# One scan instruction over two rows, with wider GpSimd products and all state groups added on GpSimd

## The chip, the cores and the metric

The kernel runs on one core of one Trainium2 chip. The metric is device microseconds of one execution; less is better. The core has a matrix engine (TensorE, PE in the profile, with its weight loads as PEld), a vector engine (VectorE, DVE), an activation engine (ScalarE, ACT), GpSimd (POOL) and SyncE (SP), which here issues the DMAs. Each engine works through its own instructions in order, and they wait for each other by semaphores. SBUF is the working memory, PSUM the memory that TensorE writes to; a PSUM bank here is 128 partitions by 512 fp32 numbers.

## The reference

A block in three steps on `x` of 4 sequences, 1024 positions and 512 features, all fp32: half a feed-forward network, a state-space layer with a selective scan, half of the same feed-forward network again. Each has a layer norm in front and a residual around it.

```python
x = x + 0.5 * ffn(layernorm(x))
x = x + mamba(layernorm(x))
x = x + 0.5 * ffn(layernorm(x))

def ffn(x):                                   # inner width 1408
    g = (x @ gate_w.T) * gate_s
    u = (x @ up_w.T) * up_s
    return ((silu(g) * u) @ down_w.T) * down_s

def mamba(x):                                 # I = 1024 channels, N = 16 states
    h, gate = split(W_in @ x)
    h = silu(causal_conv(h, 4 taps) + conv_b)
    ts, Bm, Cm = split(Wx @ h, [128, 144])    # each rms-normed
    delta = softplus(Wdt @ ts + dt_bias)
    for t in positions:                       # per channel i and state n
        s = exp(delta[t] * A) * s + delta[t] * Bm[t] * h[t]
        y[t] = sum over n of s * Cm[t]
    y = (y + D * h) * silu(gate)
    return Wout @ y
```

## The kernel before

**Tiling.** The positions are cut into 16 chunks of T = 256 (NCS = 16, four to a sequence). A chunk of the state-space layer has NI = 8 blocks of 128 channels. For the scan a block is laid out anew: S = 4 rows side by side in the free dimension, each of 128 partitions that hold 32 channels (Q = 32) times 4 states, and NS = 4 state groups g, so that 4 x 4 states of a block come to 16 rows of 256 positions. The feed-forward passes run over 512 positions at a time (the first and last over 256), in an order written out by hand (`ORDER`), and are placed between the chunks' work.

**Order of the instructions.** The program first builds a list of operations with an engine, a cost, a due time and the buffers they read and write. `Plan.run` then places them in a model of the five engines, the earliest that can start first and, among those, the one with the earliest due time (`HOT` is always first); this fixes the order on every engine and which buffer slot each one takes. Due times of chunk k come from `at(k, unit)`, with `PACE` us to a chunk and 32 units in it. `SLOTS` says how many buffers a class has: `mm` the PSUM banks of all matrix products (4), `da` the PSUM banks of the scan (3), `px` the products (14 of two rows), `rep` the spread delta and delta*h (2). One further bank, `yps`, holds the output of the fold.

**One step of the scan** (function `scan`; for each chunk k, block i, group g and pair of rows h = 0 or 2):
- ScalarE writes exp(delta * A) of each of the two rows into `da`, 128x256 each, with `A` as a pointer operand (line 841).
- GpSimd multiplies the spread delta*h with B for the pair, 128x512, into `sb` (line 848).
- VectorE runs one `tensor_tensor_scan` for each row, 128x256 (line 857), which starts from `state`, or from 0 in the first chunk of a sequence; it then copies the two last columns into `state` (line 867, not in the last chunk of a sequence) and multiplies the pair with C, 128x512, into `sb` (line 874).
- After an odd group, GpSimd adds the pair to that of the group before, 128x512 (line 882). Two summed groups for each pair of rows remain for a block.
- TensorE folds them: 8 fp32 products with a 128x32 matrix `fold` (16 instructions, as each fp32 product is two), four column groups of 32 into `yps` (line 891). VectorE adds D*h (line 903), GpSimd multiplies with the gate (line 909).

**Around it.** `normed` makes a layer norm of one tile of 128 positions: VectorE the statistics (lines 332, 333), GpSimd three small operations for 1/sqrt and the bias (lines 337 to 339), ScalarE the scaling (line 350), TensorE four transposes (line 343), ScalarE the copy out (line 358). `ffn` makes the gate and up products (line 414), whose banks ScalarE (line 429) and VectorE (line 452) empty; the down product of the full passes is split by a Strassen scheme, whose sums of halves GpSimd makes (`combine`, line 506). `prep` makes the input projection (line 633, `hp`), the four taps of the convolution (ScalarE line 668, VectorE line 676), the small projection `sp` and its rms norm (ScalarE squares line 706, GpSimd powers lines 710 to 712, VectorE line 717). `heads` makes delta (ScalarE softplus line 772, GpSimd line 784) and writes it to memory and back, spread over the partitions, by the DMAs `row` and `rep`. `gates` makes the gating products (line 633, `gp`), which ScalarE copies out (line 812). `tail` makes the output projection (line 930). Silu and softplus need other activation tables than exp, so each goes with two table loads.

Of the kernel before, what the change touches and what calls it, by code (L numbers as in the profile page):

```python
# [37 lines left out]
for _p in range(7, 14, 2):  # L38
# [3 lines left out]
SLOTS = dict(  # L42
    mm=4, da=3, rf=12, rm=6, px=14, xf=4, xi=2, xo=1, xn=3, ss=2, sm=8, sr=4, u=2, dd=2, rep=2, bc=2, sn=2, sq=1, row=8, bcd=2, tsT=1, bcT=1, xnT=1,
)
PACE = 153
# [6 lines left out]
HOT = -1e9  # L52

# [126 lines left out]
def macaron_kernel(ctx: ExitStack, tc: tile.TileContext, a: dict, out: bass.AP):  # L180
# [7 lines left out]
    yps = banks.tile([P, 2, T], F32, name="yps")  # L188
    ident = const.tile([P, P], F32, name="ident")
    make_identity(nc, ident)  # L190
    neg_half = const.tile([P, 4], F32, name="neg_half")
    nc.gpsimd.memset(neg_half, -0.5)
    fold = const.tile([P, Q], F32, name="fold")
# [40 lines left out]
    def mm(name):  # L234
        return Buf("mm", name, [P, 512])
# [44 lines left out]
    def scale_down(down, due):  # L280
        ds2 = Buf("px", "ds2", [P, 2, T])

        def flat():
            return ds2.tile.rearrange("p a t -> p (a t)")
# [35 lines left out]
    def normed(x, at_x, name, due, flipped):  # L320
        sm = Buf("sm", f"sm{name}", [P, 16])
        xn = Buf("xn", f"xn{name}", [P, H])
        tp = mm(f"tp{name}")
        m, q = (sm, 0), (sm, 1)

        def parts():
            s = sm.tile
            return s[:, 0:6], s[:, 6:8], s[:, 8:9], s[:, 9:10], s[:, 10:11]

        def spread():  # L330
            stt, mv, *_ = parts()
            pin(nc.vector.bn_stats(stt, at_x()))
            pin(nc.vector.bn_aggr(mv, stt))

        def roots():
            _, mv, ve, rs, nb = parts()
            pin(nc.gpsimd.tensor_scalar(ve, mv[:, 1:2], EPS, None, ALU.add))
            pin(nc.gpsimd.tensor_tensor(rs, ve, neg_half[:, 0:1], ALU.pow))
            pin(nc.gpsimd.tensor_scalar(nb, mv[:, 0:1], rs, -1.0, ALU.mult, ALU.mult))

        def turned():
            for k in range(KH):
                pin(nc.tensor.transpose(tp.tile[:, k * P : (k + 1) * P], xn.tile[:, k * P : (k + 1) * P], ident))

        dst, w, more = flipped
        op("DVE", 0.65, spread, x, [m], due - 9, name=f"stats{name}")
        op("POOL", 1.0, roots, [m], [q], due - 8, name=f"roots{name}")
        op(
            "ACT", 0.71,
            lambda: pin(nc.scalar.activation(  # L350
                xn.tile, at_x(), AF.Identity, bias=sm.tile[:, 10:11], scale=sm.tile[:, 9:10],
            )),
            list(x) + [q], [xn] + w, due - 4, name=f"xn{name}",
        )
        op("PE", 0.45, turned, [xn], [tp], due - 2, name=f"flip{name}")

        def out_of():
            pin(nc.scalar.copy(dst(), tp.tile.rearrange("p (k t) -> p k t", k=KH)))  # L358
            if more:
                more()  # L360

        op("ACT", 0.48, out_of, [tp], w, HOT, name=f"unflip{name}")

# [18 lines left out]
    def ffn(n):  # L382
# [13 lines left out]
        for v, (stage, p) in enumerate(of):  # L396
            x = x_of[p] if stage == 2 and p in x_of else Buf("xf", f"x{name}_{v}", [P, 2, H])
            pairs.append(x)
            for m in range(J):
                t, r = J * v + m, J * p + m  # L400
                due = ffn_due(base[0]) - FLIPS - 3 * (W4 - t)
                if x.cls == "xf":
                    src, key = (a["x"][r * P : (r + 1) * P, :], ()) if stage == 1 else (x2[r], [("x2", r)])
                    behind("xf", move(
                        lambda x=x, m=m, src=src: dma(x.tile[:, m, :], src), 256, key, quads(x, m), due - 16, after=last_of("xf"), name=x.name,
                    ))
                normed(
                    quads(x, m), lambda x=x, m=m: x.tile[:, m, :], f"{name}_{t}", due,
                    (lambda t=t: fxT[:, :, t * P : (t + 1) * P], [("fxT", t)], None),
                )  # L410
# [11 lines left out]
        for it in range(NF):  # L422
# [9 lines left out]
                [gp], [("hd", it, t) for t in ts], HOT, name=f"ungate{name}_{it}",  # L432
# [55 lines left out]
    def split_down(name, tiles, pairs, spend):  # L488
# [21 lines left out]
        for r0, r1 in ((0, 3), (3, K1)):  # L510
# [5 lines left out]
            combine(v1, a21, a22, ALU.add, h_of(r0, r1, 1) + h_of(q0, q1, 1), s_of(s1, r0, r1), n, t0 - 4 + r0, "s1")  # L516
            combine(v2, v1, a11, ALU.subtract, h_of(r0, r1, 0) + s_of(s1, r0, r1), s_of(s2, r0, r1), n, t0 + 3 + r0, "s2")
            combine(a21, a11, a21, ALU.subtract, h_of(r0, r1, 0) + h_of(r0, r1, 1), h_of(r0, r1, 1), n, t0 + 8 + r0, "s3")
# [85 lines left out]
        for r0, r1 in ((0, 3), (3, K1)):  # L604
# [3 lines left out]
                ALU.subtract, h_of(q0, q1, 0) + s_of(s2, r0, r1), h_of(q0, q1, 0), r1 - r0, t0 + 15 + r0, "s4",  # L608
# [31 lines left out]
    def prep(k):  # L640
        d = st[k]
        base = at(k - 1, 7) if k else 70.0
        xT = d["xnT"] = Buf("xnT", f"xnT{k}", [P, KH, K - 1 + T])
        for j in range(J):
# [4 lines left out]

            def edges(j=j):  # L650
# [7 lines left out]
            o = K - 1 + j * P  # L658
            normed([x], lambda x=x: x.tile, f"m{k}_{j}", base + 2 * j, (lambda o=o: xT.tile[:, :, o : o + P], [(xT, j)], None))
            op("POOL", 0.3, edges, [(xT, 1)] if j else [], [("back",)] if j else [(xT, 0), ("back",)], HOT, name=f"edges{k}_{j}")  # L660
        u = d["u"] = Buf("u", f"u{k}", [P, NI, T])
        for i in range(NI):
# [9 lines left out]
            op("ACT", 0.45, first, [hp], [(u, i)], HOT, name=f"tap{k}_{i}")  # L672
# [16 lines left out]
        sr = [Buf("sr", f"sr{k}_{j}", [P, 8]) for j in range(J)]  # L689
# [12 lines left out]
        for j in range(J):  # L702
            def squares(j=j):
                v = sp.tile.rearrange("p (j t) -> p j t", j=J)
                for q, (o, m) in enumerate(parts):
                    pin(nc.scalar.activation(sq.tile[:, o : o + m], v[:, j, o : o + m], AF.Square, accum_out=sr[j].tile[:, q : q + 1]))

            def powers(j=j):
                ss, rr = sr[j].tile[:, 0:3], sr[j].tile[:, 4:7]
                pin(nc.gpsimd.tensor_scalar(ss[:, 0:1], ss[:, 0:1], 1.0 / R, EPS, ALU.mult, ALU.add))  # L710
                pin(nc.gpsimd.tensor_scalar(ss[:, 1:3], ss[:, 1:3], 1.0 / N, EPS, ALU.mult, ALU.add))
                pin(nc.gpsimd.tensor_tensor(rr, ss, neg_half[:, 0:3], ALU.pow))

            def weigh(j=j):
                v = sp.tile.rearrange("p (j t) -> p j t", j=J)
                for q, (o, m) in enumerate(parts):
                    pin(nc.vector.scalar_tensor_tensor(
                        sn[j].tile[:, o : o + m], v[:, j, o : o + m], sr[j].tile[:, 4 + q : 5 + q], ln_w[:, o : o + m], ALU.mult, ALU.mult,
                    ))

            op("ACT", 0.6, squares, [sp], [sq, (sr[j], 0)], HOT, name=f"sq{k}_{j}")
            op("POOL", 1.4, powers, [(sr[j], 0)], [(sr[j], 1)], HOT, name=f"rr{k}_{j}")
            op("DVE", 0.54, weigh, [sp, (sr[j], 1)], [sn[j]], HOT, name=f"sn{k}_{j}")
# [82 lines left out]
    def gates(k):  # L806
        for i in range(NI):
# [5 lines left out]
                [gp], [("g", i)], HOT, name=f"ung{k}_{i}",  # L813
# [7 lines left out]
    def scan(k):  # L821
# [4 lines left out]
        for i in range(NI):  # L826
# [4 lines left out]
            for g in range(NS):  # L831
                due = at(k, i * NS + g)
                for h in range(0, S, 2):
# [3 lines left out]
                    sb = Buf("px", f"sb{nm}", [P, 2, T])  # L837
                    for j in range(2):
# [7 lines left out]
                    behind("dbu", op(  # L846
                        "POOL", 1.23,
                        lambda sb=sb, h=h, g=g, rep=rep: pin(nc.gpsimd.tensor_tensor(  # L848
                            sb.tile, rep.tile[:, h : h + 2, 1, :], bc.tile[:, g : g + 1, :].to_broadcast([P, 2, T]), ALU.mult,
                        )),  # L850
                        reps + bcs, [(sb, 0), (sb, 1)], due - 6, after=last_of("dbu"), name=f"dbu{nm}",
                    ))
                    for j in range(2):
                        key = ("state", i, g, h + j)
                        op(
                            "DVE", 0.582 if first else 0.642,
                            lambda da=da, sb=sb, j=j, h=h, g=g, b0=b0: pin(nc.vector.tensor_tensor_scan(  # L857
                                da.tile[:, j, :], da.tile[:, j, :], sb.tile[:, j, :],
                                0.0 if first else state[:, b0 + h + j, g : g + 1], ALU.mult, ALU.add,
                            )),  # L860
                            [(da, j), (sb, j)] + ([] if first else [key]), [(da, j)], due, after=last_of("scan"), name=f"scan{nm}_{j}",
                        )
                        behind("scan", plan.ops[-1])
                    if not last:
# [9 lines left out]
                        lambda sb=sb, da=da, g=g: pin(nc.vector.tensor_tensor(  # L874
                            sb.tile, da.tile, bc.tile[:, NS + g : NS + g + 1, :].to_broadcast([P, 2, T]), ALU.mult,
                        )),
                        [(da, 0), (da, 1)] + bcs, [(sb, 0), (sb, 1)], due, name=f"prod{nm}",
                    )
                    if g % 2:
                        pa = made_of[g - 1 + h // 2]  # L880
                        op(
                            "POOL", 1.23, lambda pa=pa, sb=sb: pin(nc.gpsimd.tensor_tensor(pa.tile, pa.tile, sb.tile, ALU.add)),  # L882
                            [(pa, 0), (pa, 1), (sb, 0), (sb, 1)], [(pa, 0), (pa, 1)], due + 2, name=f"both{nm}",
                        )
                    else:
                        made_of.append(sb)
# [168 lines left out]
```

## Time and profile before

| | us |
|---|---|
| median of 3 runs | 2821.67 (2821.48 to 2822.98) |
| the profiled execution | 2822.59 |
| its span | 2820.8 |
| PE busy | 2768.3 (98%) |
| DVE busy | 2543.7 (90%) |
| POOL busy | 2395.0 (85%) |
| ACT busy | 1756.3 (62%) |
| DMA engines, mean busy share by slice | 5 to 8 tenths until slice 38 |

The mean granted TensorE clock is 0.994. Instructions of one engine overlap by some tens of nanoseconds in the records, so the distance from one start to the next is a little less than the duration; busy time counts each instant once. In the groups, a line of the kernel stands with engine, operation, output and inputs, shape and count, then busy time and mean duration in ns, then the idle time before it with what ended it. The scan runs from 153 us (first exp) to about 2723 us (last sum).

The groups that the state scan consists of:

```profile
L841 ACT ACTIVATE da<-rep,a_w 128x256 f32<-128x256 f32 x2048 | 964.7, 476 | 794.8 <-DVE sb L874 734.4
L848 POOL TENSOR_TENSOR sb<-rep,bc 128x512 f32<-128x512 f32 x1024 | 1284.1, 1280 | 81.5 <-DMA rep<-row 59.2
L857 DVE TENSOR_TENSOR_SCAN da<-da,state,sb 128x256 f32<-128x256 f32 x1536 | 1090.8, 741 | 49.6 <-ACT da L841 29.5
L882 POOL TENSOR_TENSOR sb<-sb,sb 128x512 f32<-128x512 f32 x512 | 651.5, 1278 | 84.9 <-DVE sb L874 83.1
L874 DVE TENSOR_TENSOR sb<-da,bc 128x512 f32<-128x512 f32 x1024 | 692.8, 677 | 0.5
```

### The profile page before, as it was taken

To read this page: it belongs to the slowest core of one execution; us is meant where nothing else is said; L and a number is where in the kernel's file an instruction comes from. 1 tells how busy PE (TensorE), PEld (TensorE's weight loads), DVE (VectorE), ACT (ScalarE), POOL (GpSimd) and SP (SyncE) were. 2 spreads that over 40 slices of the span, in tenths; PEclk is the share of its full clock that TensorE was granted. 3 is DMA by queue.
4 is the path that set the end of the run, shared out by engine and by line. 5 is a ranking of instruction groups with operands and counts; after the bars stand their busy time and mean duration, and the time that the engine had idled before them with its cause. 6 is when DMAs were issued, how large, how long until landed. Compare 5 with 4: busy or idle time off the path is not lost.

```text
span 2820.8 us, 38816 instructions
## 1 busy us (share of the span) xinstructions
PE 2768.3 (98%) x11278; PEld 1733.2 (61%) x11278; DVE 2543.7 (90%) x5088; ACT 1756.3 (62%) x3286; POOL 2395.0 (85%) x2279
## 2 busy tenths in 40 slices
PE   8998999999999999999999999999999999999999
PEld 6565575575655755647557565575665756657458
DVE  3289899999999999999999999999999999999861
ACT  2356667667567585676666766668567576674821
POOL 1189899899898989899899999899899998989951
PEclk9999999999999999999999999999999999999999
DMA  8576667676576666866757667666676775766635
GB/s 263 168 206 178 168 184 219 185 214 197 148 236 158 202 185 172 233 160 189 206 162 236 168 185 207 196 175 194 173 224 173 219 208 153 211 165 176 175 102 155
DMA packets 304691, 531.01 MB, mean 188 GB/s; under 512 B 34016, under 2 KB 58720, under 8 KB 304480
## 3 DMA queue, kind: packets, MB, share of 16 engines
q1 hardware_dynamic: 303040, 528.35, 66.5%
q8 instruction: 90, 1.47, 0.2%
q14 instruction: 121, 0.99, 0.1%
q10 hardware_dynamic: 1440, 0.19, 0.0%
HBM read 464.84 MB, written 63.57 MB: 187 GB/s over the span
## 4 chain that ended last, share of the span: by engine, by line
PE 43%; DVE 35%; issue 7%; ACT 7%; POOL 5%; DMA 3%; SPq 0%; ACTq 0%; DVEq 0%; POOLq 0%
DVE da L857 21%; PE upf L414 11%; PE gatef L414 11%; DVE sb L874 6%; PE hp L633 3%; PE gp L633 3%; PE op L930 2%; PE paf L539 2%; POOL sb L848 2%; ACT da L841 2%; DVE u L676 2%; PE yps L891 2%; PE pcf L539 2%; DMA rep<-row 2%; PE pbf L539 1%
## 5 line engine op out<-in xcount | busy, mean ns | idle before, releaser
L841 ACT ACTIVATE da<-rep,a_w 128x256 f32<-128x256 f32 x2048 | 964.7, 476 | 794.8 <-DVE sb L874 734.4
L848 POOL TENSOR_TENSOR sb<-rep,bc 128x512 f32<-128x512 f32 x1024 | 1284.1, 1280 | 81.5 <-DMA rep<-row 59.2
L857 DVE TENSOR_TENSOR_SCAN da<-da,state,sb 128x256 f32<-128x256 f32 x1536 | 1090.8, 741 | 49.6 <-ACT da L841 29.5
L882 POOL TENSOR_TENSOR sb<-sb,sb 128x512 f32<-128x512 f32 x512 | 651.5, 1278 | 84.9 <-DVE sb L874 83.1
L874 DVE TENSOR_TENSOR sb<-da,bc 128x512 f32<-128x512 f32 x1024 | 692.8, 677 | 0.5
L414 PE MATMUL gatef<-fxT,w_gate_w 128*128 128x512 f32 (+1 forms) x1496 | 632.7, 574 | 5.1 <-ACT dd L772 3.0
L414 PE MATMUL upf<-fxT,w_up_w 128*128 128x512 f32 (+1 forms) x1496 | 624.3, 569 | 0.5 <-DVE u L676 0.5
L414 PEld LDWEIGHTS gatef<-fxT,w_gate_w 128*128 128x128 f32 x1496 | 284.5, 192 | 294.7 <-issue 267.6
L414 PEld LDWEIGHTS upf<-fxT,w_up_w 128*128 128x128 f32 x1496 | 280.9, 190 | 290.9 <-issue 268.0
L857 DVE TENSOR_TENSOR_SCAN da<-da,sb 128x256 f32<-128x256 f32 x512 | 333.5, 681 | 22.6 <-ACT da L841 19.5
L633 PE MATMUL hp<-xnT,w_W_in 128*128 128x259 f32 x1024 | 238.6, 383 | 4.3 <-ACT fxT L358 1.5
L633 PE MATMUL gp<-xnT,w_W_in 128*128 128x256 f32 x1024 | 241.1, 380 | 0.2 <-ACT fxT L358 0.2
L633 PEld LDWEIGHTS hp<-xnT,w_W_in 128*128 128x128 f32 x1024 | 192.4, 190 | 61.3 <-issue 20.1
L633 PEld LDWEIGHTS gp<-xnT,w_W_in 128*128 128x128 f32 x1024 | 191.9, 189 | 61.0 <-issue 28.4
L930 PE MATMUL op<-w_Wout,u 128*128 128x512 f32 x512 | 229.3, 594 | 0.0
L452 DVE SCALAR_TENSOR_TENSOR hd<-upf,up_s,hd 128x512 f32<-128x512 f32 (+1 forms) x187 | 131.0, 701 | 59.4 <-PE upf L414 59.4
L676 DVE SCALAR_TENSOR_TENSOR u<-hp,conv_w,u 128x256 f32<-128x256 f32 x384 | 171.9, 468 | 6.0 <-ACT u L668 5.3
L429 ACT ACTIVATE hd<-gatef,gate_s 128x512 f32<-128x512 f32 (+1 forms) x187 | 121.8, 652 | 64.0 <-PE gatef L414 63.8
L930 PEld LDWEIGHTS op<-w_Wout,u 128*128 128x128 f32 x512 | 95.8, 190 | 105.2 <-issue 99.4
L891 PE MATMUL yps<-sb,fold 128*32 128x256 f32 x2048 | 141.1, 387 | 0.6 <-POOL sb L882 0.5
L539 PE MATMUL paf<-w_half,hd 128*128 128x256 f32 x620 | 141.0, 380 | 0.0
L539 PEld LDWEIGHTS paf<-w_half,hd 128*128 128x128 f32 x620 | 117.1, 190 | 22.0 <-issue 4.4
(104 smaller groups left out, 2911.1 us busy)
## 6 DMA issues: line engine op xcount, KB each, us to landing
rep<-row SPq DMA_DIRECT2D x512, 256.0 KB, 5.0
w_half<-sd SPq DMA_DIRECT2D x272, 256.0 KB, 3.0
w_W_in<-in_W_in_dram SPq DMA_DIRECT2D x256, 256.0 KB, 3.9
w_gate_w<-in_gate_w_dram SPq DMA_DIRECT2D x187, 256.0 KB, 4.5
w_up_w<-in_up_w_dram SPq DMA_DIRECT2D x187, 256.0 KB, 3.6
row<-dd SPq DMA_DIRECT2D x128, 256.0 KB, 3.2
w_Wout<-in_Wout_dram SPq DMA_DIRECT2D x128, 256.0 KB, 3.8
bc<-bcd SPq DMA_DIRECT2D x64, 256.0 KB, 5.2
```

What stands on the lines that cost most here:

```text
L414: pin(nc.tensor.matmul(o.tile[:, :wide], lhsT=cols(w.tile)[:, k, :], rhs=fxT[:, k, :wide], start=(k == 0), stop=(k == KH - 1),))
L452: lambda up=up, it=it: pin(nc.vector.scalar_tensor_tensor(hd[:, it, :wide], up.tile[:, :wide], up_s[:, it : it + 1], hd[:, it, :wide], ALU ...
L539: pin(nc.tensor.matmul(bank.tile[:, m * hh : (m + 1) * hh], lhsT=of(r, m), rhs=w.tile[:, h * hh : (h + 1) * hh], start=(first and m == 0 a ...
L633: pin(nc.tensor.matmul(o.tile[:, :width], lhsT=cols(w.tile)[:, kk, :], rhs=xT.tile[:, kk, lo:], start=(kk == 0), stop=(kk == KH - 1),))
L676: lambda hp=hp, i=i, q=q: pin(nc.vector.scalar_tensor_tensor(u.tile[:, i, :], hp.tile[:, q : q + T], conv_w[:, i, q : q + 1], u.tile[:, i, ...
L841: lambda da=da, j=j, h=h, g=g, rep=rep, b0=b0: pin(nc.scalar.activation(da.tile[:, j, :], rep.tile[:, h + j, 0, :], AF.Exp, scale=a_w[:, b ...
L848: lambda sb=sb, h=h, g=g, rep=rep: pin(nc.gpsimd.tensor_tensor(sb.tile, rep.tile[:, h : h + 2, 1, :], bc.tile[:, g : g + 1, :].to_broadcas ...
L857: lambda da=da, sb=sb, j=j, h=h, g=g, b0=b0: pin(nc.vector.tensor_tensor_scan(da.tile[:, j, :], da.tile[:, j, :], sb.tile[:, j, :], 0.0 if ...
L874: lambda sb=sb, da=da, g=g: pin(nc.vector.tensor_tensor(sb.tile, da.tile, bc.tile[:, NS + g : NS + g + 1, :].to_broadcast([P, 2, T]), ALU. ...
L882: "POOL", 1.23, lambda pa=pa, sb=sb: pin(nc.gpsimd.tensor_tensor(pa.tile, pa.tile, sb.tile, ALU.add)),
L891: pin(nc.tensor.matmul(yps[j * Q : (j + 1) * Q, i % 2, :], lhsT=fold, rhs=made_of[2 * g + j // 2].tile[:, j % 2, :], start=(g == 0), stop= ...
L930: pin(nc.tensor.matmul(o.tile, lhsT=u.tile[:, i, j * P : (j + 1) * P], rhs=wo[i].tile, start=(i == 0), stop=(i == NI - 1),))
```

## The change

- **Scan.** The two rows of a pair become one scan of 512 columns over `da`, with 0 as its start. So that the second row does not go on from the first, the first column of each row of `da` is set to zero by a ScalarE copy (`opened`). In chunks that go on from a state, ScalarE first puts exp * state + product into the first column of `sb`, one small activation for each row.
- **Products.** GpSimd multiplies all four rows of a group at once, 128x1024. Pair sums are 1024 wide too, and one more GpSimd addition per block (`all`) adds the two sums that are left. The fold is 4 products (8 instructions) for a block, and takes a bank of class `mm`; `yps` is gone. `da` has 4 banks, `px` 8 buffers of four rows.
- **Norms.** `normed` takes two tiles at a time: VectorE adds epsilon, GpSimd makes one power for both, ScalarE makes the bias in two small activations. In `prep`, ScalarE scales the sums of squares and adds epsilon, and GpSimd makes one power for both tiles.
- **Order.** `PACE` is 150 instead of 153. The copies out of the product banks on ScalarE are due 20 us before their product's due time (`EV`) rather than first of all; the GpSimd half sums of the split down product are due 16 us earlier (`SUMS`); the output projection's matmuls are cut into four parts rather than two.

```diff
-    mm=4, da=3, rf=12, rm=6, px=14, xf=4, xi=2, xo=1, xn=3, ss=2, sm=8, sr=4, u=2, dd=2, rep=2, bc=2, sn=2, sq=1, row=8, bcd=2, tsT=1, bcT=1, xnT=1,
-PACE = 153
+SLOTS = dict(mm=4, da=4, rf=12, rm=6, px=8, xf=4, xi=2, xo=1, xn=3, ss=2, sm=6, sr=2, u=2, dd=2, rep=2, bc=2, sn=2, sq=1, row=8, bcd=2, tsT=1, bcT=1, xnT=1)
+PACE = 150
...
+SUMS = 20
+EV = 20
...
-    yps = banks.tile([P, 2, T], F32, name="yps")
...
-    def normed(x, at_x, name, due, flipped):
+    def normed(name, pair):
+        sm = Buf("sm", f"sm{name}", [P, 2, 16])
 
         def roots():
-            _, mv, ve, rs, nb = parts()
-            pin(nc.gpsimd.tensor_scalar(ve, mv[:, 1:2], EPS, None, ALU.add))
-            pin(nc.gpsimd.tensor_tensor(rs, ve, neg_half[:, 0:1], ALU.pow))
-            pin(nc.gpsimd.tensor_scalar(nb, mv[:, 0:1], rs, -1.0, ALU.mult, ALU.mult))
+            v = sm.tile
+            pin(nc.gpsimd.tensor_tensor(v[:, :, 9], v[:, :, 8], neg_half[:, 0:2], ALU.pow))
+
+        for j, (x, at_x, due, _) in enumerate(pair):
+            def spread(j=j, at_x=at_x):
+                s = sm.tile[:, j, :]
+                pin(nc.vector.bn_stats(s[:, 0:6], at_x()))
+                pin(nc.vector.bn_aggr(s[:, 6:8], s[:, 0:6]))
+                pin(nc.vector.tensor_scalar(s[:, 8:9], s[:, 7:8], EPS, None, ALU.add))
...
+            def scaled(j=j, at_x=at_x, xn=xn):
+                s = sm.tile[:, j, :]
+                pin(nc.scalar.activation(s[:, 10:11], s[:, 6:7], AF.Identity, scale=s[:, 9:10]))
+                pin(nc.scalar.activation(s[:, 11:12], s[:, 10:11], AF.Identity, scale=-1.0))
+                pin(nc.scalar.activation(xn.tile, at_x(), AF.Identity, bias=s[:, 11:12], scale=s[:, 9:10]))
...
-                [gp], [("hd", it, t) for t in ts], HOT, name=f"ungate{name}_{it}",
+                [gp], [("hd", it, t) for t in ts], due - EV, name=f"ungate{name}_{it}",
...
-            combine(v1, a21, a22, ALU.add, h_of(r0, r1, 1) + h_of(q0, q1, 1), s_of(s1, r0, r1), n, t0 - 4 + r0, "s1")
+            combine(v1, a21, a22, ALU.add, h_of(r0, r1, 1) + h_of(q0, q1, 1), s_of(s1, r0, r1), n, t0 - SUMS + r0, "s1")
...
-                    pin(nc.scalar.activation(sq.tile[:, o : o + m], v[:, j, o : o + m], AF.Square, accum_out=sr[j].tile[:, q : q + 1]))
+                    at_q = sr.tile[:, 0, j, q : q + 1]
+                    pin(nc.scalar.activation(sq.tile[:, o : o + m], v[:, j, o : o + m], AF.Square, accum_out=at_q))
+                    pin(nc.scalar.activation(at_q, at_q, AF.Identity, bias=eps, scale=1.0 / m))
...
+                sb = Buf("px", f"sb{k}_{i}_{g}", [P, S, T])
+                behind("dbu", op(
+                    "POOL", 2.31,
+                    lambda sb=sb, g=g, rep=rep: pin(nc.gpsimd.tensor_tensor(
+                        sb.tile, rep.tile[:, :, 1, :], bc.tile[:, g : g + 1, :].to_broadcast([P, S, T]), ALU.mult,
+                    )),
+                    reps + bcs, [(sb, j) for j in range(S)], due - 7, after=last_of("dbu"), name=f"dbu{k}_{i}_{g}",
+                ))
...
+                    def opened(da=da, sb=sb, h=h, g=g, b0=b0):
+                        for j in range(0 if first else 2):
+                            pin(nc.scalar.activation(
+                                sb.tile[:, h + j, 0:1], da.tile[:, j, 0:1], AF.Identity,
+                                bias=sb.tile[:, h + j, 0:1], scale=state[:, b0 + h + j, g : g + 1],
+                            ))
+                        pin(nc.scalar.copy(da.tile[:, :, 0], zeros))
+
+                    op("ACT", 0.08 if first else 0.23, opened, keys + ([] if first else hs), [(da, 0), (da, 1)] + ([] if first else hs), due - 3, name=f"open{nm}")
+                    op(
+                        "DVE", 1.12,
+                        lambda da=da, sb=sb, h=h: pin(nc.vector.tensor_tensor_scan(
+                            da.tile.rearrange("p a t -> p (a t)"), da.tile.rearrange("p a t -> p (a t)"),
+                            sb.tile[:, h : h + 2, :].rearrange("p a t -> p (a t)"), 0.0, ALU.mult, ALU.add,
                         )),
...
+            pa, pb = made_of
+            op(
+                "POOL", 2.31, lambda pa=pa, pb=pb: pin(nc.gpsimd.tensor_tensor(pa.tile, pa.tile, pb.tile, ALU.add)),
+                [(b, j) for b in (pa, pb) for j in range(S)], [(pa, j) for j in range(S)], at(k, (i + 1) * NS) + 3, name=f"all{k}_{i}",
+            )
+            yp = mm(f"yp{k}_{i}")
+
+            def summed(yp=yp, pa=pa):
+                if True:
                     for j in range(S):
                         pin(nc.tensor.matmul(
-                            yps[j * Q : (j + 1) * Q, i % 2, :], lhsT=fold, rhs=made_of[2 * g + j // 2].tile[:, j % 2, :],
-                            start=(g == 0), stop=(g == NS // 2 - 1),
+                            yp.tile[j * Q : (j + 1) * Q, :T], lhsT=fold, rhs=pa.tile[:, j, :], start=True, stop=True,
                         ))
...
-            for lo in (0, NI // 2):
-                hi = lo + NI // 2
+            for lo in range(0, NI, 2):
+                hi = lo + 2
```

## The prediction

> **What bounds the kernel now.** I read the busy times by stretch first, then the waits of each engine, then the groups by form, and last the timeline for the distance between starts. The stretch from 150 to 2700 us holds the state scan and all but the first and last matmul passes:
>
> ```profile
> core 0: us, PE busy (x) PEld busy (x) DVE busy (x) ACT busy (x) POOL busy (x), PEclk, DMA share, GB/s
> 0.00:150.00 150.00, 140.19 (x498) 92.27 (x499) 46.91 (x108) 45.86 (x75) 18.76 (x53) 1.00 0.70 216
> 150.00:2700.00 2550.00, 2511.62 (x10277) 1551.16 (x10276) 2457.78 (x4913) 1691.70 (x3179) 2346.10 (x2196) 0.99 0.68 189
> 2700.00:2821.00 121.00, 116.49 (x507) 89.74 (x505) 39.03 (x69) 18.74 (x33) 30.13 (x31) 1.00 0.42 128
> ```
>
> In those 2550 us PE is busy 98.5%, DVE 96.4%, POOL 92.0%, ACT 66.3%. PE lacks 38 us in all, and its longest single cause in that stretch is 9.9 us of waiting for POOL's half sums. So TensorE ends the stretch, with VectorE just behind; both must shrink for a gain. The other engines' waits in the same stretch:
>
> ```profile
> ACT da L841 <- DVE sb L874: 726.7, 662, 3.5
> ...
> POOL sb L882 <- DVE sb L874: 78.7, 68, 4.6
> POOL sb L848 <- DMA rep<-row: 59.2, 25, 14.7
> ...
> DVE da L857 <- ACT da L841: 49.0, 44, 4.2
> ```
>
> The columns are total us, times, longest. ScalarE waits because it runs ahead and finds no free exp bank: that is spare time. GpSimd's waits are the ones to remember, because the change loads GpSimd.
>
> **TensorE: the fold halves.** One fold is 16 matmuls now, 8 after, since the two remaining state-group sums are added on GpSimd first.
>
> ```profile
> 1226.13 1.07 PE L891 MATMUL yps<-sb,fold 128*32 128x256 f32 x16
> 1227.13 3.27 PE L414 MATMUL gatef<-fxT,w_gate_w 128*128 128x512 f32 x7
> ```
>
> Sixteen take 1.00 us from start to the next start, though one lasts 387 ns in the groups: the four column groups run side by side, in four waves. From 1.07 and 0.387 a wave is (1.07 - 0.387) / 3 = 0.23 us, so two waves last 0.62 and hold PE for 0.55. Saved: 0.45 x 128 = 58 us; if it scaled straight, 64. I take 58. The result moves from a bank of its own to one of the four that all matmuls share, for some 0.55 + 0.46 us (fold and line 903). I cost this at nothing: the other three banks take 3 x 3.5 us of gate products, 10 us of cover; without it each fold could hold PE for that 1 us, 128 us in all. PE needs 2511.6 - 58 = 2454 us; with its 38 us of idle time kept, the stretch is 2492.
>
> **VectorE: one scan for two rows.**
>
> ```profile
> 1211.47 0.68 DVE L874 TENSOR_TENSOR sb<-da,bc 128x512 f32<-128x512 f32 x1
> 1212.07 0.75 DVE L857 TENSOR_TENSOR_SCAN da<-da,state,sb 128x256 f32<-128x256 f32 x1
> 1212.73 0.46 DVE L903 SCALAR_TENSOR_TENSOR u<-u,d_w,yps 128x256 f32<-128x256 f32 x1
> ```
>
> and from the groups by form (busy, mean of one in ns, idle before it):
>
> ```profile
> L857 DVE TENSOR_TENSOR_SCAN da<-da,sb 128x256 f32<-128x256 f32 x512 | 333.5, 681 | 22.6 <-ACT da L841 19.5 <-POOL sb L848 1.2
> ```
>
> A scan with a state operand holds the engine 0.66 us, one without about 0.06 less (681 against 741 ns), 0.60. A 512-wide scan is not in the trace. Least: the slope of the plain products (677 - 418 ns for 256 columns, 1.01 ns each) gives 0.60 + 0.26 = 0.86. Most: no gain, 1.20. A 256-wide scan lasts 681 against 418 for a product, 263 more, which is a second nanosecond per column; so I take 2.05 ns, and 0.60 + 0.53 = 1.13. Pairs: 768 x (1.32 - 1.13) + 256 x (1.20 - 1.13) = 164 us saved; 347 at the least price, 92 at the most. Added: one 1-column operation per normalized tile, 96 x about 0.1 (the 99 ns between the two statistics operations) = 10. DVE falls to 2458 - 154 = 2304, 92.5% of 2492.
>
> **GpSimd: fewer, wider, but one more add.** Its form rows are 128x256 732 ns, 128x512 1284, 128x768 1825: 2.11 to 2.16 ns per column. 1024 wide is then 2.37 us, less 0.02 of overlap (1284.1 / 1024 against 1280). Now: 1284.1 + 651.5 = 1935.6. After, per block of 128 channels, 4 products, 2 pair sums and 1 last sum: 896 x 2.35 = 2106. That is +170. Roots: 102 us of three operations for each of 96 tiles become 48 powers two columns wide; one column is 571 ns, three 861, so 716 x 48 = 34: -68. The powers of the inner norm: 39.7 become 16 x 1.3 (six columns by the same slope) = 21: -19. Sum +83, so 2346 + 83 = 2429 in the stretch, **97.5% of 2492**. Two-column and six-column powers could cost from one-column to no saving; that moves 20 us.
>
> The Trainium skill (GPSIMD Engine Reference, Key points) says elementwise work is structurally about twice as fast on VectorE, and so speaks against this part. This trace agrees (1280 ns against 677 for 128x512); by the rule the last sum would sit on VectorE for about 128 x 1.2 = 154 us, with GpSimd at 2128 and VectorE at 2458.
>
> **ScalarE: the first columns.** Per pair of rows it gains a two-element copy, and in the 12 chunks of 16 that go on from a state two one-column affine operations with two pointer operands each. No such small one is in the trace. Rows: copy 366 ns, one pointer (line 772) 474, two pointers (line 668) 556, all 256 wide; line 429 gives 676 at 512 and 471 at 256, 0.80 ns per column, 205 for 256. So the fixed parts are 0.16 and 0.35 us; consecutive ones overlap 0.11 (four of line 772 take 1.57 us, so they stand 0.365 apart). Least: 768 x (2 x 0.24 + 0.05) + 256 x 0.05 = 420 us. Most, no overlap: 768 x 0.86 + 256 x 0.16 = 701. I take the least, since ACT's dependent squares already follow each other in the timeline without waiting. With 96 x 0.2 for the normalization and 96 x 0.14 for the squares, +33. ACT: 1692 + 453 = 2145, 86% of 2492; 2426 at most.
>
> The Trainium skill (ScalarE: Activation LUTs, What ACT_TABLE_LOAD costs) gives 186 ns plus 93 per pointer operand with 93 ns of overlap, from which an estimate for these operations is 527 us instead of 420. The trace's steps of 108 and 82 ns per pointer are near it; ACT would stand at 2252.
>
> A new wait comes with this: the column operation needs GpSimd's product. Behind it in ACT's queue stand the next exps and the evictions of gate, conv and gating products (lines 429, 668, 812), for which PE's four banks wait. Cover: products are due 7 us ahead of their scan, the column operation 3 us, and the banks give 10 us.
>
> **What costs nothing.** The number of DMAs is unchanged, so the rep queue on SP stays and its 59 us of GpSimd waits too. Exp banks go from three to four, which only helps ACT, that has 727 us of such waits. Paired normalization holds the first tile for the second: hidden by passes planned far ahead, but open at the end, where the flip before the last gate products follows the last add; about +1 us. The last sum lengthens the final fold by 2.3 us, under 30 us of other PE work (2727 to 2757 in the chain of waits). Priorities and pace have no price by themselves.
>
> **Sum.** The profiled run took 2822.6 (span 2820.8 and 1.8 around it), 0.9 above the median. PE alone: 2822.6 - 58 = 2765. GpSimd cannot be busy 97.5% with the waits above; VectorE shows that an engine not at the end of everything reaches 96.4% here. Between that and PE's 98.5% I take 97%: 2429 / 0.97 = 2504, 46 us less than 2550. Forecast **2777 us**.
>
> **Rivals.**
>
> *GpSimd becomes the bound and loses time (slower, 0.22).* It is in order; each pair sum waits for VectorE's last product, each gating for line 903, which now waits for a longer chain: sum, last sum, fold. It breaks even at 2429 / 2550 = 95.3%. At 94% the stretch is 2584: 2857. For it: at present it is only 92% busy, and the waits on DVE and on rep are 138 us. Against: part of those are waits of an engine that is early.
>
> *ScalarE starves the scan (slower, 0.13).* Table switches with their work block exps for 1.28 + 1.91 + 1.28 = 4.5 us, some 100 times (42 + 32 + 15 + 12). Four banks hold 4 x (1.13 + 0.06 + 0.60) = 7 us, but refilling one costs ACT 2 x 0.46 + 0.53 = 1.45 us against VectorE's 1.79, so it recovers slowly. If the small operations cost the upper 701 us, ACT needs 2426, and at a 94% share 2581 us: 2854. It decides from 95.1% upwards. Against: the 2145 I take leaves 14%.
>
> *The order keeps the waits (no change, 0.08).* PE's freed 58 us turn into waits at folds placed by a plan: 2822. Against: PE waited 0.5 us for folds' sums before.
>
> **Numbers.** Forecast case 0.57, its own range 2745 (PE also regains half of its 38 us) to 2810. Overall 2745 to 2857, the top from GpSimd at 94%. Within 0.2% is about what this kernel's runs cannot tell from no change: 0.06; faster 0.57 + 0.02 of the last rival = 0.59; slower 0.35.
>
> **What would show it.** Right: fold x8 at about 0.55 us apart, 512-wide scans 1.1 apart, PE still at 98% or more, POOL at 96 to 97.5% with fewer waits on DVE. Wrong: PE waiting for POOL's sums at folds, DVE waiting for ACT for more than 150 us, 1024-wide POOL operations above 2.45 us, small ACT operations above 0.3 apart.

## The result, and the profile after

The changed kernel takes 2898.29 us (median of 4 runs, 2895.55 to 2899.18) against 2822.32 in runs beside it: 1.0267 of the time before, 95% interval 1.025 to 1.0285. The profiled execution took 2899.18, its span is 2897.1. The forecast was 2777.

The busy times by stretch (us of each engine, number of instructions in brackets):

```profile
core 0: us, PE busy (x) PEld busy (x) DVE busy (x) ACT busy (x) POOL busy (x), PEclk, DMA share, GB/s
0.00:150.00 150.00, 139.27 (x495) 91.48 (x496) 48.72 (x119) 51.84 (x97) 9.13 (x20) 1.00 0.67 214
150.00:2780.00 2630.00, 2497.24 (x9283) 1527.62 (x9282) 2333.16 (x3993) 2264.53 (x6005) 2458.60 (x1281) 0.98 0.64 184
```

The scan's stretch has grown from about 2550 to 2630 us and no engine fills it: PE 95.0%, POOL 93.5%, DVE 88.7%, ACT 86.1%. VectorE and TensorE have less to do than before and stand idle more. The groups (busy us, mean ns, idle before them and its causes):

```profile
L872 DVE TENSOR_TENSOR_SCAN da<-da,sb 128x512 f32<-128x512 f32 x1024 | 1219.0, 1221 | 244.0 <-ACT da L867 230.7
L841 POOL TENSOR_TENSOR sb<-rep,bc 128x1024 f32<-128x1024 f32 x512 | 1209.0, 2372 | 43.6 <-DMA rep<-row 37.7
L854 ACT ACTIVATE da<-rep,a_w 128x256 f32<-128x256 f32 x2048 | 940.2, 472 | 231.5 <-DVE sb L889 207.3
...
L863 ACT ACTIVATE sb<-da,sb,state 128x1 f32<-128x1 f32 x1536 | 449.9, 343 | 42.2 <-POOL sb L841 30.0
...
L905 POOL TENSOR_TENSOR sb<-sb,sb 128x1024 f32<-128x1024 f32 x128 | 303.3, 2369 | 1.3
...
L867 ACT COPY da<-zeros 128x2 f32<-128x2 f32 x1024 | 165.3, 161 | 27.8
```

Before, scans waited 49.6 + 22.6 us in all; now 244 us, 231 of them for the column copy on ScalarE (line 867). ScalarE's own waits for a free exp bank fell from 734 to 207 us: it no longer runs ahead. In the chain of waits ScalarE now holds 33% (7% before). The scan of a pair itself takes 1.13 us from its start to that of the next operation:

```profile
1209.37 1.23 DVE L872 TENSOR_TENSOR_SCAN da<-da,sb 128x512 f32<-128x512 f32 x1
1210.50 0.47 DVE L679 SCALAR_TENSOR_TENSOR u<-hp,conv_w,u 128x256 f32<-128x256 f32 x1
```

The trace holds its own comparison. The first chunk of a sequence has no state to carry, so ScalarE does the copies there but none of the 1536 activations of line 863. The next two stretches are chunk 4, which is such a chunk, and chunk 5, which carries. Each runs from VectorE's last product with C of the chunk before to its own:

```profile
810.00:964.00 154.00, 151.46 (x544) 88.89 (x543) 147.35 (x271) 111.46 (x275) 150.48 (x80) 0.99 0.67 193
964.00:1135.00 171.00, 158.23 (x565) 92.55 (x564) 147.59 (x269) 153.47 (x416) 154.59 (x81) 0.98 0.63 180
```

Without a carry PE is busy 98.4% and GpSimd 97.7%, which is about what the prediction had asked of them; with a carry they are down to 92.5% and 90.4%. From the last product with C of one chunk to that of the next, chunks 4, 8 and 12 went from 157.2 us on average to 154.0, the eleven that carry (without the last chunk) from 162.5 to 168.4.

Of the 76 us: PE's busy time fell by 19 us only, though the fold saved 59 (141.1 to 82.1 in its row, here before and after), and PE's idle time grew by 95 (2897.1 - 2749.6 against 2820.8 - 2768.3).

```profile
L891 PE MATMUL yps<-sb,fold 128*32 128x256 f32 x2048 | 141.1, 387 | 0.6 <-POOL sb L882 0.5
```

```profile
L913 PE MATMUL yp<-sb,fold 128*32 128x256 f32 x1024 | 82.1, 392 | 21.4 <-POOL sb L905 13.2 <-ACT hd L429 2.1 <-ACT xnT L354 1.9
```

Part of the busy time that did not fall is a lower granted clock, 0.985 against 0.994: as an estimate from clock and span, 43 us missing from full speed against 17. In the place shown here it follows an idle gap:

```profile
1084.48 0.64 PE L913 MATMUL yp<-sb,fold 128*32 128x256 f32 x8
1090.53 5.66 PE L414 MATMUL upf<-fxT,w_up_w 128*128 128x512 f32 x9 [5.41 <-DVE hd L452]
```

```profile
1085.00:1090.00 5.00, 0.12 (x4) 0.00 (x0) 2.62 (x3) 4.87 (x17) 2.52 (x2) 1.00 0.65 193
1090.00:1094.00 4.00, 3.47 (x5) 1.64 (x6) 3.33 (x7) 3.95 (x8) 4.00 (x3) 0.57 0.00 0
1094.00:1100.00 6.00, 6.00 (x16) 2.65 (x15) 4.49 (x9) 5.74 (x18) 5.75 (x3) 1.00 0.44 107
```

After a gap of 5.4 us the granted clock (the number before the DMA share) is 0.57 for the next 4 us: PE pays for this stall again when it resumes. The Trainium skill (TensorE: Matmul & The Clock Gate, Part 1) says the array's clock is halved after an idle window of about 3.4 us; these rows agree. The length of the gap does not decide alone in this trace: after a gap of 2.0 us (PE resumes at 1431.11) the next 4 us had 0.57 too, and after one of 2.5 us (PE resumes at 2418.64) they had 1.00.

### The profile page after: what moved, and what is told of

It reads as the page before. It is cut to its first block, busy times and chain, and to the rows that moved or that the text cites. A ratio compares the mean times of both kernels' runs of the same rounds, so it can differ in the third digit from the quotient of the medians.

```text
span 2897.1 us, 37777 instructions
## 1 busy us (share of the span) xinstructions
PE 2749.6 (95%) x10254; PEld 1707.5 (59%) x10254; DVE 2407.8 (83%) x4160; ACT 2329.4 (80%) x6125; POOL 2492.9 (86%) x1321
## 4 chain that ended last, share of the span: by engine, by line
ACT 33%; PE 29%; DVE 20%; POOL 10%; issue 5%; DMA 3%; SPq 0%; ACTq 0%; POOLq 0%; DVEq 0%
DVE da L872 10%; ACT da L854 9%; PE upf L414 9%; ACT sb L863 6%; PE gatef L414 5%; DVE sb L889 4%; POOL sb L841 4%; ACT L1016 3%; DVE u L679 3%; POOL sb L897 2%; PE gp L633 2%; PE pcf L539 2%; PE paf L539 2%; ACT hd L440 2%; ACT hd L429 2%
## 5 line engine op out<-in xcount | busy, mean ns | idle before, releaser
L872 DVE TENSOR_TENSOR_SCAN da<-da,sb 128x512 f32<-128x512 f32 x1024 | 1219.0, 1221 | 244.0 <-ACT da L867 230.7
L841 POOL TENSOR_TENSOR sb<-rep,bc 128x1024 f32<-128x1024 f32 x512 | 1209.0, 2372 | 43.6 <-DMA rep<-row 37.7
L854 ACT ACTIVATE da<-rep,a_w 128x256 f32<-128x256 f32 x2048 | 940.2, 472 | 231.5 <-DVE sb L889 207.3
L897 POOL TENSOR_TENSOR sb<-sb,sb 128x1024 f32<-128x1024 f32 x256 | 606.7, 2370 | 74.3 <-DVE sb L889 38.1
L414 PE MATMUL gatef<-fxT,w_gate_w 128*128 128x512 f32 (+1 forms) x1496 | 641.3, 581 | 27.3 <-ACT hd L429 18.6
L414 PE MATMUL upf<-fxT,w_up_w 128*128 128x512 f32 (+1 forms) x1496 | 634.0, 575 | 20.3 <-DVE hd L452 7.4
L863 ACT ACTIVATE sb<-da,sb,state 128x1 f32<-128x1 f32 x1536 | 449.9, 343 | 42.2 <-POOL sb L841 30.0
L905 POOL TENSOR_TENSOR sb<-sb,sb 128x1024 f32<-128x1024 f32 x128 | 303.3, 2369 | 1.3
L867 ACT COPY da<-zeros 128x2 f32<-128x2 f32 x1024 | 165.3, 161 | 27.8
```

The costliest lines, as they stand in the source:

```text
L414: pin(nc.tensor.matmul(o.tile[:, :wide], lhsT=cols(w.tile)[:, k, :], rhs=fxT[:, k, :wide], start=(k == 0), stop=(k == KH - 1),))
L841: lambda sb=sb, g=g, rep=rep: pin(nc.gpsimd.tensor_tensor(sb.tile, rep.tile[:, :, 1, :], bc.tile[:, g : g + 1, :].to_broadcast([P, S, T]), ...
L854: lambda da=da, j=j, h=h, g=g, rep=rep, b0=b0: pin(nc.scalar.activation(da.tile[:, j, :], rep.tile[:, h + j, 0, :], AF.Exp, scale=a_w[:, b ...
L863: pin(nc.scalar.activation(sb.tile[:, h + j, 0:1], da.tile[:, j, 0:1], AF.Identity, bias=sb.tile[:, h + j, 0:1], scale=state[:, b0 + h + j ...
L872: lambda da=da, sb=sb, h=h: pin(nc.vector.tensor_tensor_scan(da.tile.rearrange("p a t -> p (a t)"), da.tile.rearrange("p a t -> p (a t)"), ...
L897: "POOL", 2.31, lambda pa=pa, sb=sb: pin(nc.gpsimd.tensor_tensor(pa.tile, pa.tile, sb.tile, ALU.add)),
```

## The experiments

The theory after the result: ScalarE cannot deliver the columns in time, because the plan that orders all engines was told 0.23 us for the three column operations of a pair (0.40 for an exp). In the profile the second activation starts 0.24 us after the first, the copy 0.37 us later and what follows 0.10 us later still, so that a pair takes about 0.72 us from start to start (an exp 0.40 to 0.51):

```profile
1211.55 0.59 ACT L863 ACTIVATE sb<-da,sb,state 128x1 f32<-128x1 f32 x2
1212.17 0.16 ACT L867 COPY da<-zeros 128x2 f32<-128x2 f32 x1
1212.27 0.56 ACT L671 ACTIVATE u<-hp,conv_b,conv_w 128x256 f32<-128x256 f32 x1
```

The rivals: the work itself is too much whatever the order, or GpSimd's last sum is the bound. Most experiments are single runs; where a kernel was run four or five times, the runs lie 0.1 to 0.3% apart. "True costs" below means 0.455 us for an exp and, for the column operations of a pair, 0.72 us with a carry, 0.47 with half of it and 0.10 without.

**The plan told the measured costs.** Same instructions, another order.

```diff
-                            "ACT", 0.4,
+                            "ACT", 0.455,
-                    op("ACT", 0.08 if first else 0.23, opened, ...
+                    op("ACT", 0.10 if first else 0.72, opened, ...
```

> The changed kernel with the same instructions, ordered by a plan that knows their measured distances: exp 0.455 us instead of 0.40, the column operations of a pair 0.72 instead of 0.23 (0.10 instead of 0.08 without a state). If ScalarE's work itself is the cause: 2880 to 2900 us, VectorE still waits over 180 us for the column copies. If only the order made from too low costs is the cause: 2765 to 2830 us. If GpSimd's sums are the cause: within 10 us of 2898.

2825.75 us: 73 of the 76 us are gone with no instruction changed, so the order was the main cause. VectorE's waits for the copy fell from 231 to 147 us in the scan's stretch (the columns are total us, times, longest), and PE idles 100 us of the span instead of 147.

```profile
DVE da L872 <- ACT da L867: 230.7, 158, 4.5
```

```profile
DVE da L872 <- ACT da L867: 146.5, 102, 5.0
```

> The changed kernel, with only the plan's cost of the column operations set to the measured distance (0.72 and 0.10 instead of 0.23 and 0.08); exps stay at 0.40. If that one misjudged cost makes the order bad: 2815 to 2840 us, as with both costs set (2825.8). If the exps' 0.055 us too little (2048 of them) matters as much: 2855 us or more. If any shift of the order would do: no telling, both may fall.

2834.30 us: the one number of the column operations brings 64 us of it.

> The changed kernel with the plan's exp at 0.455 us and the column operations of a pair at 1.10 us, more than the 0.72 measured. If the gain of true costs (2899 to 2826) comes from their being true: 2835 us or more, worse again. If any rearrangement, or more reserve for ScalarE, does as well: 2815 to 2830 us.

2934.63 us. A cost that is 0.38 us too high loses more than one that is 0.49 us too low, so neither just any shift of the order nor more reserve for ScalarE brings the gain. The loss is another one: VectorE's waits for the copy are down to 88 us, but PE idles 170 us of the span. Between 0.23, 0.72 and 1.10 no value was tried, so it is not shown that the measured cost is the best one.

> The kernel before, with the plan's cost of an exp 0.455 instead of 0.40 and nothing else. ScalarE has over 700 us of spare waiting there, so if misjudged costs hurt only an engine that is near full: 2815 to 2830 us. If the order gains from any truer cost: 2800 us or less.

2817.53 us beside 2822.02, the same within what single runs tell. Before the change, where ScalarE had room, an exp that was 0.055 us too cheap in the plan cost at most some 4 us.

**The parts alone.** Two scans per pair again, without the column operations; then the column copies without the carry; then the pair scan alone in the kernel before.

```diff
 # e2                       two scans of 256 columns with their start operand, no opened()
 # e3
-                        for j in range(0 if first else 2):
+                        for j in range(0):
 # e4                       the kernel before with opened() at its 0.23 us and the 512-column scan
```

> The changed kernel with the two scans per pair of before, without ScalarE's column operations; 1024-wide products, the last sum on GpSimd, four exp banks, paired norms and priorities stay. If ScalarE is the cause: 2765 to 2825 us, VectorE's waits for exps fall from 231 to under 80 us. If GpSimd is the cause: 2860 us or more, with PE waiting for the last sums.

> The changed kernel with the column copies alone: the state isn't carried into a chunk, so the 1536 one-column activations are left out. If they are the cause: every chunk takes the 154 us that the first chunks of a sequence take now, and the time falls to 2750 to 2790 us. If GpSimd is the cause: 2860 us or more.

> The kernel before with the paired scan and ScalarE's column operations alone (three exp banks, 512-wide products, the fold of 16, priorities of before). If ScalarE is the cause: 2870 to 2920 us. If GpSimd's last sum is the cause: 2780 to 2822 us, since VectorE saves some 150 us.

2817.83, 2774.83 and 2909.27 us. With two scans VectorE is the bound again, 2487.5 of 2550 us (97.5%), so that TensorE's 58 us bring only some 6. VectorE's waits for exps are down to 7 us. The paired scan with its carry costs 85 us in the old surroundings too, so neither the last sum nor the wide products are needed for the loss. Without the activations the change takes the time that was forecast (2777), even with an exp at 0.40 in the plan:

```profile
core 0: us, PE busy (x) PEld busy (x) DVE busy (x) ACT busy (x) POOL busy (x), PEclk, DMA share, GB/s
150.00:2650.00 2500.00, 2453.50 (x9267) 1517.33 (x9266) 2327.19 (x3993) 1827.38 (x4467) 2454.61 (x1281) 0.99 0.68 193
```

That is PE 98.1% and GpSimd 98.2% at once: GpSimd can be driven that full. The 1536 activations are worth 123 us in the order as changed, and 51 in the order with true costs, both against this run, whose plan makes an order of its own.

**What the remaining 51 us are.** Load, wait, or GpSimd:

```diff
 # e10: the activation writes to a place that nobody reads, without waiting for the product
-                                sb.tile[:, h + j, 0:1], da.tile[:, j, 0:1], AF.Identity,
+                                junk[:, j : j + 1], da.tile[:, j, 0:1], AF.Identity,
 # e11: no op named "all"; the fold multiplies both sums
 # e12
-PACE = 150
-SUMS = 20
+PACE = 153
+SUMS = 4
-                [gp], ..., due - EV, ...
+                [gp], ..., HOT, ...
```

> The changed kernel with both plan costs as measured; ScalarE makes all 1536 one-column activations, but writes them to a place that nobody reads and doesn't wait for GpSimd's product, so the state isn't carried. It tells ScalarE's load from its wait for the product. If the load remains the cost: 2815 to 2830 us, as with the carry (2825.8). If the wait for the product in ScalarE's queue is the cost: 2770 to 2790 us, as without the activations (2774.8).

2828.97 us: with the activations' wait for the product taken away nothing is gained, so this wait is not the cost. ScalarE's load is left as one that may be.

> The changed kernel with both plan costs as measured and without the last sum on GpSimd: the fold takes 8 products (16 instructions) again, GpSimd has 300 us less to do. If GpSimd is what keeps the version with true costs at 2826: 2800 us or less. If TensorE and ScalarE are: TensorE's 58 us come back, 2830 to 2880 us.

2812.61 us, less than with the last sum although TensorE has its 59 us of fold work back. Expected was either 2800 or less, or more than 2830; it lies between. In the scan's stretch:

```profile
150.00:2680.00 2530.00, 2494.26 (x10267) 1543.17 (x10266) 2342.34 (x3992) 2227.28 (x5985) 2168.77 (x1154) 1.00 0.68 191
```

GpSimd is down to 85.7%, ScalarE still at 88.0%, and TensorE is the bound again at 98.6%. A loaded GpSimd could be borne in e3 and a loaded ScalarE can here; that the two together are what keeps e1 from the forecast is argued from this, not shown.

> The changed kernel without the last sum on GpSimd, with the change's own plan costs (0.23 and 0.40). If ScalarE's misjudged cost is a cause by itself: 2870 us or more, some 60 above the same with true costs (2812.6). If it hurts only together with a full GpSimd: 2830 us or less.

2902.45 us, 90 more than with true costs: the misjudged costs act by themselves, with GpSimd relieved.

> The changed kernel with both plan costs as measured, and the pace, the due times of the half sums and the rank of the copies out of the product banks as before (153, 4 us ahead, first of all). If the new priorities matter: 2840 us or more. If the order is made by the costs alone: 2815 to 2835 us.

2845.95 us, 20 more than with the new priorities: with true costs these help a little, so nothing speaks for their having a part in the loss.

**Less work for ScalarE.** All three have true costs in the plan. First half of the work is taken away: the first row of a pair starts from its state in the scan, and only the second is set up. Then the whole carry of a block is made with one exp of 128x16, with the additions on VectorE (e8 and e9 are told in short, not as their code).

```diff
 # e7
-                        for j in range(0 if first else 2):
+                        for j in range(2 if first else 1, 2):
-                        pin(nc.scalar.copy(da.tile[:, :, 0], zeros))
+                        pin(nc.scalar.copy(da.tile[:, 1, 0:1], zeros[:, 0:1]))
-                            sb.tile[...], 0.0, ALU.mult, ALU.add,
+                            sb.tile[...], 0.0 if first else state[:, b0 + h, g : g + 1], ALU.mult, ALU.add,
 # e8
+                ec.tile = a_w[:, b0 : b0 + S, :] * rep.tile[:, :, 0, 0:1]     (VectorE; e9: GpSimd)
+                ec.tile = exp(ec.tile) (ScalarE; e9: into PSUM), then times state (VectorE)
+                    sb.tile[:, :, 0] += ec.tile[:, :, g]                      (VectorE, for each group)
```

> The changed kernel with both plan costs as measured, and half of ScalarE's column work: the first row of a pair starts from its state by the scan's own start operand, so that ScalarE sets up only the second row (768 activations instead of 1536, one-element copies). VectorE pays 0.06 us for 768 scans. If the remaining loss is ScalarE's work: half of the 51 us between the version with true costs and the one without a carry comes back, 2790 to 2810 us. If it isn't: 2820 us or more.

2819.24 us: 6 us better than with the whole carry, where 16 to 36 were expected. ScalarE's busy time fell by 150 us (2291.0 to 2141.1), so its load alone does not explain the 51 us.

> The changed kernel with both costs as measured, and the carry made in one go for a block: VectorE multiplies A with the first delta for all 16 rows (128x16), ScalarE makes one exp of them, VectorE multiplies with the states and adds the result to the first columns of a group's four rows; ScalarE is left with the one-element copies. If ScalarE's work is what remains: 2770 to 2795 us, as without a carry, and ScalarE below 1900 us busy. If the wait for the carry itself is what costs: 2815 us or more.

3130.01 us, far above what was expected of less work for ScalarE, and not for the reason that stood beside "2815 us or more": scans wait only 34 us. VectorE is busy 97.8% from 150 to 3000 us. The three small operations of the carry, each with both inputs in SBUF, take 337, 115 and 66 us of it. The next run moves one of them to GpSimd and gives the other two an input in PSUM:

> The batched carry again, arranged so that no VectorE operation has two inputs in SBUF: GpSimd makes the product with the first delta, ScalarE writes the exps to PSUM, and VectorE's small operations take one input from there; one exp bank fewer (3) makes the room. If VectorE's 128x4 additions took 0.9 us in the version before because GpSimd was running: they now take under 0.3 us, and the time falls from 3130 to 2770 to 2810 us. If they are slow by themselves or the order is bad: over 2850 us.

2883.68 us. The row of the addition, first with both inputs in SBUF, then with one in PSUM:

```profile
L858 DVE TENSOR_TENSOR sb<-sb,ec 128x4 f32<-128x4 f32 x384 | 337.0, 894 | 0.5
```

```profile
L860 DVE TENSOR_TENSOR sb<-sb,ecb 128x4 f32<-128x4 f32 x384 | 51.0, 159 | 49.9 <-POOL sb L854 48.3
```

894 ns became 159, and the operation of 66 us took 16.5. The time did not come down to the 2770 to 2810 expected: this version has one exp bank fewer and new waits (ScalarE 45 us for GpSimd's small product, VectorE 44 us for the wide ones), and which of them matters was not tried.

**A version that beats both.** True costs and the half carry of e7, in e16 with no last sum as in e11, in e17 with it for every other block:

```diff
 # e17
+            if i % 2:
+                op("POOL", 2.31, ... pa + pb ..., name=f"all{k}_{i}")
+                made_of = [pa]
```

> True costs, no last sum on GpSimd, and half of ScalarE's column work (the first row of a pair starts from its state in the scan). If TensorE alone bounds the version without the last sum (98.6% busy at 2812.6): 2800 to 2812 us, nothing much to gain. If ScalarE still costs: 2780 to 2800 us.

> As the run before, but the last sum goes to GpSimd for every other block: TensorE is spared 29 us, GpSimd pays 150. If the loads of GpSimd and ScalarE are what eats TensorE's 58 us: 2775 to 2800 us, the best of all that carry the state. If the last sum is bad wherever it stands: 2812 us or more.

2811.82 us, 0.9961 of the kernel before (0.9947 to 0.9975), and 2802.63 us, 0.9930 (0.9915 to 0.9945). Both gains are small, but their intervals lie below 1. In the first, with TensorE as the bound, ScalarE's relief buys nothing (2812.61 without it). The second, slightly above its expected range, trades part of TensorE's work against part of GpSimd's and is the fastest of these versions that carries the state.

## Why the prediction was wrong, by its own steps

- **The fold**: 0.62 us and 58 us forecast; 0.64 and 59 (141.1 - 82.1) measured. Right, but the time went into PE's gaps.
- **The scan**: 1.13 us from start to start forecast; the timeline has the same (1209.37 to 1210.50). VectorE's 2304 us came out as 2333 in the longer stretch. Right, though the saving at the least price was added up wrongly: 768 x 0.46 + 256 x 0.34 is 440 us, not 347. The forecast does not use that figure.
- **GpSimd**: 2.37 us forecast, 2372 and 2369 ns measured; 2429 us forecast, 2459 measured. Right. It was not thought able to be 97.5% busy; it reaches 98.2% when nothing is carried (e3).
- **ScalarE**: 0.53 us for a pair's column operations, taken at the lower bound; 0.72 measured, since the copy starts 0.37 us after the second activation instead of 0.24, and holds ScalarE for 0.10 instead of 0.05. From start to start these operations come to 768 x 0.72 + 256 x 0.10 = 579 us where 420 stood. 2145 us forecast for ScalarE, 2265 measured: too low by 120, inside the upper bound. The estimate of 527 us that the prediction worked out from the Trainium skill (ScalarE: Activation LUTs, What ACT_TABLE_LOAD costs) was nearer than 420, and low too.
- **The step that failed** is the order put at nothing ("Priorities and pace have no price by themselves"), and with it the step of the sum that rests on it, "Between that and PE's 98.5% I take 97%" for GpSimd, with ScalarE's free 14% as cover. GpSimd came to 93.5%, of 2630 us. The diff tells the plan 0.23 us for an operation that the prediction itself priced at 0.53. Against the measured 0.72, 768 of them hide some 376 us of ScalarE work from the plan, and 2048 exps at 0.40 instead of 0.455 another 113. The order then places copies, exps and evictions as if ScalarE were early. The longest wait of a scan for its copy was 4.5 us, more than the 3 us of cover. The prediction compared busy sums with the stretch and never set the plan's costs against its own. e1 and e5 show this by taking 73 and 64 us off with no instruction changed, e14 by costing 90 us with GpSimd relieved. The due times and the pace, which the sentence names, did no harm by themselves (e12).
- **What stays open**: true costs do not reach the forecast, 2825.75 us is 49 above it. Leaving out the 1536 activations brings about as much, 51, so ScalarE's free 14% was not free. Taking half of this work off ScalarE brought only 6 us (e7), leaving out the last sum 13 (e11); which waits make up the rest is not settled.
- **The rivals**: "ScalarE starves the scan" names the place rightly (DVE waiting for ACT above 150 us was its sign: 231), at 0.13 far too small a chance, and with the wrong condition: it was to decide from 95% of ScalarE's time, and did so at 86%. "The order keeps the waits" looked at the waits of PE for sums at the folds alone; those came to 13 us, and the price of the order lay in ScalarE's queue. "GpSimd becomes the bound" is not what lost the time (e14, e4); that GpSimd's load takes a part of the gain is suggested by e11 and e17.

## What to carry to other kernels

Where the order of the instructions comes from a list of costs, an operation's cost in that list is part of the kernel: compare each new one with a start-to-start distance in a trace before judging the operation. A tiny instruction costs its fixed part: the three column operations took ScalarE 0.72 us for a pair of rows, where the start operand of two scans had cost VectorE some 0.12 us, so moving a per-row start to another engine can cost more than it saves. Work freed on the bounding engine did not become time here: four engines at 86 to 95% took longer than PE at 98% and VectorE at 96% beside GpSimd at 92% and ScalarE at 66%.

## What the hardware showed unexpectedly

- A VectorE addition of 128x4 with both inputs in SBUF took 894 ns on average and up to 7.7 us while GpSimd was working, and 159 ns with one input in PSUM. The Trainium skill (SBUF — State Buffer, Who interferes with whom) says that a VectorE instruction with two SBUF inputs contends with a GpSimd instruction that reads SBUF, since its second input comes through a read interface that the two share; e8 and e9 agree.
- A PE gap of 5.4 us was followed by 4 us at 0.57 of the clock, so that this stall weighed more than its length. Over the whole span the granted clock was 0.994 before, 0.985 after, 0.972 in e13.
- A two-element ScalarE copy, which overwrites columns that the two activations ahead of it have read, started 0.37 us after the second of them, 0.03 us after its end; the second activation had started 0.24 us after the first, 0.10 us before its end. Why the copy did not overlap is not shown.
